# The order of three products in layer 0's LSTMs, and the engine of one copy

## The chip, the cores and the metric

One core of a Trainium2 chip runs the whole program. Its engines work side by side, each through its own queue of instructions: TensorE (PE in the profile, its weight loads PEld), VectorE (DVE), ScalarE (ACT), GpSimd (POOL), and the queues that issue DMAs (SP among them). Semaphores order what depends on another engine. The metric is the device time of one execution in microseconds; the time before is the median of three runs.

## The reference, cut to what matters

A stack of four graph layers works on x of shape (128, 64, 256): 128 sequences of 64 nodes with 256 features. The change lies in layer 0, in its LSTMs:

```python
for p in range(1, MAX_SKIP + 1):                     # MAX_SKIP = 4
    nw = Tv // p
    wins = h[:, :nw * p, :].reshape(Bv * nw, p, Hd)  # windows of p nodes
    last = _lstm_last(Wih[p - 1], Whh[p - 1], bih[p - 1], bhh[p - 1], wins)
    idx = jnp.arange(nw) * p + (p - 1)
    h = h.at[:, idx, :].set(last.reshape(Bv, nw, Hd))

def step(carry, x_t):                                # in _lstm_last
    h, c = carry
    g = x_t @ Wih.T + h @ Whh.T + bias
    i, f, gg, o = jnp.split(g, 4, axis=-1)
    c = sigmoid(f) * c + sigmoid(i) * tanh(gg)
    h = sigmoid(o) * tanh(c)
```

For each window length p = 1 to 4 an LSTM runs over windows of p nodes, from a zero state, and its last hidden state replaces the window's last node. The next p reads what the one before has written. Features and hidden state have 256 elements each, and a gate is a 256x256 product with x, and one with h from the second step on. All is in float32.

## The kernel before

**The work of the LSTMs.** Nodes stand in the free dimension, features in the partitions, in two blocks of 128. Nodes are split into two halves u as well, so a gate is a 2x2 by 2x2 block product. It is done with seven block products in place of eight (a Strassen scheme): `Weights` and `prepare` make sums of weight blocks and of input blocks, and numbers 1 to 7 name the products. `w` is the window length p. The batch goes in two halves of 64 sequences; in each, w runs from 1 to 4 (a phase), and a phase is cut into parts: four parts of N = 512 columns for w=1, four of 256 for w=2, two of 336 for w=3 and two of 256 for w=4. Two parts go hand in hand: step t of the one, then step t of the other. A step with t = 0 (a first step) has three gates (i, g, o) and takes one matmul a product; later steps have four (i, g, f, o) and two matmuls a product, the second with h. There are 24 + 48 + 112 = 184 gates: 8 steps of w=1, 16 first steps of w=2 to 4, 28 later steps. The program's order of matmuls is kept as it is written; for the other engines a scheduler, which works when the program is built, places independent instructions.

**A gate** (`gate`, a generator) yields three times and so has four parts:
- A: products 1 into `pa` and 2 into `pb`; ScalarE copies `pa` out (L684), VectorE adds `pb` (L685), ScalarE applies the function (in `func`, L669).
- B: product 6 onto `pa`, copied by ScalarE (L689); product 7 into `pc`, copied by ScalarE (L691): the third partial sum, block (1, 1).
- C: product 5 onto `pa`, which has to wait until L689 has read it; VectorE adds `pa` to the copied `pc` (L694).
- D: product 3 onto `pa`, which has to wait until L694 has read it, and a function straight from it; product 4 onto `pc`, added by VectorE (L699); a function on both remaining blocks; then `gate_done`.

PSUM has three banks for `pa`, three for `pc` and two for `pb`, which are also used to transpose a finished group (`group_out`, with the residual add L170).

`gate_done` multiplies i by g (L709, or L720 in a first step), updates c (L717, L718), takes its tanh (L721), and after the o gate makes h (L739) with the sums of its blocks (L741 to L743), or writes the result back to hT (L726 for w=1, L734 for a last step). `prepare` makes the next step's inputs: copies by ScalarE (L622, L623), subtractions by VectorE (L624, L630, L631; L613, L617, L618 for w=1). GpSimd makes the sums of the weight blocks in line 432.

**The loop over gates** is a software pipeline. In each slot one gate is new, the one before it is the middle gate (`flight[-1]`), and the one before that is the oldest:

```python
            if len(flight) > 1:
                next(flight[-1][1])          # middle gate: part C
                old = flight.pop(0)
                next(old[1], None)           # oldest gate: part D
```

Ahead of this the new gate does A, after it B. TensorE's order in a slot is so 1, 2 (new), 5 (middle), 3, 4 (oldest), 6, 7 (new).

Of the kernel before, what the change touches and what calls it, by code (L numbers as in the profile page):

```python
# [30 lines left out]
def gnn_stack_kernel(ctx: ExitStack, tc: tile.TileContext, a: dict, out: bass.AP):  # L31
    nc = tc.nc
# [24 lines left out]
    def token_tiles(ap, n=0):  # L57
        return ap[n * CHUNK : (n + 1) * CHUNK, :].rearrange("(i p) d -> p i d", p=P)
# [347 lines left out]
    with ExitStack() as l0:  # L406
# [178 lines left out]
        class Step:  # L585
# [90 lines left out]
            def gate(self, q):  # L676

                N = self.N
                pa = psl.tile([P, 512], F32, tag="pa", name="pa", bufs=3)
                pb = psl.tile([P, 512], F32, tag="bank", name="pb", bufs=2)  # L680
                pc = psl.tile([P, 512], F32, tag="pc", name="pc", bufs=3)
                self.product(q, ((1, pa, True), (2, pb, True)))
                blk, second = self.new_gate(q)
                nc.scalar.copy(blk[0, 0], pa[:, :N])  # L684
                nc.vector.tensor_tensor(blk[0, 0], pb[:, :N], blk[0, 0], ALU.add)  # L685
                self.func(q, blk[0, 0], blk[0, 0], 0)
                yield
                self.product(q, ((6, pa, False),))
                nc.scalar.copy(blk[1, 0], pa[:, :N])  # L689
                self.product(q, ((7, pc, True),))  # L690
                nc.scalar.copy(blk[1, 1], pc[:, :N])  # L691
                yield
                self.product(q, ((5, pa, False),))
                nc.vector.tensor_tensor(blk[1, 1], pa[:, :N], blk[1, 1], ALU.add)  # L694
                yield
                self.product(q, ((3, pa, False),))
                self.func(q, blk[0, 1], pa[:, :N], 0)
                self.product(q, ((4, pc, False),))
                nc.vector.tensor_tensor(blk[1, 0], pc[:, :N], blk[1, 0], ALU.add)  # L699
                self.func(q, second, second, 1)  # L700
                self.gate_done(q)
# [57 lines left out]
        def fetch_x(n):  # L759
            xt = xres.tile([P, 4, D], F32, tag="xres", name="xres")  # L760
            nc.sync.dma_start(out=xt, in_=token_tiles(a["x"], n))
            return xt
# [3 lines left out]
        def group_out(g, c):  # L766

            for u in range(2):
                n = 4 * g + 2 * u + c
                xt = residual.pop(n)  # L770
                for ip in range(2):
                    add_transposed(xt, 2 * ip, hTs0[g % 2][:, u], c * CHUNK + ip * 256)
                nc.gpsimd.dma_start(out=token_tiles(xa[n]), in_=xt)
                if g < 2:
                    m = n + NCH // 2
                    nc.sync.dma_start(
                        out=hTs0[g][:, u, :, c * CHUNK : (c + 1) * CHUNK], in_=hmem[m]
                    )

        def first_norms1(norms):  # L780

            for step in range(8):
                if step < 4:
                    for i in range(2):
                        norms[step // 2].stats(step % 2 * 2 + i)
                    if step % 2:
                        norms[step // 2].roots()
                else:
                    for i in range(2):
                        norms[step // 2 - 2].scaled(step % 2 * 2 + i)  # L790
                yield

        def phase_over(ph):

            if ph + 2 < len(phases):
                later_weights.append((slot + 8, ph + 2))
            nxt = ph + 1 if ph + 1 < len(phases) and phases[ph + 1] > 1 else ph + 2
            if phases[ph] > 1 and nxt < len(phases):
                weights["hh", nxt] = Weights("hh", phases[nxt])
# [3 lines left out]
        flight = []  # L803
# [3 lines left out]
        for slot in range(len(tasks) + 2):  # L807
            new = tasks[slot] if slot < len(tasks) else None
            if new:
                step = steps[new[0]]  # L810
                one = step.gate(new[1])
                next(one)
            if len(flight) > 1:
                next(flight[-1][1])
                old = flight.pop(0)
                next(old[1], None)
            elif flight and not new:
                old = flight.pop(0)
                next(old[1], None)
            else:  # L820
                old = None
                if flight:
                    next(flight[-1][1])
            if new:
                next(one)
                flight.append((new, one))
                at, k = new[0], new[2]
                while outs and outs[0][0] <= slot:
                    group_out(*outs.pop(0)[1:])

                new_half = at + 1 < len(steps) and at and steps[at + 1].w == 1 < step.w
                if k == len(step.gates) - (1 if new_half else 2) and at + 1 < len(steps):
                    steps[at + 1].prepare()
                if step.w == MAX_SKIP and step.t == 2 and k < 2:
                    for u in range(2):
                        n = 4 * step.g + 2 * u + k
                        later.append((slot, "x", n))
            while later and later[0][0] <= slot:
                _, kind, n = later.pop(0)
                residual[n] = fetch_x(n)  # L840
            next(norm_steps, None)
            while later_weights and later_weights[0][0] <= slot:
                _, ph = later_weights.pop(0)
                weights["ih", ph] = Weights("ih", phases[ph])
            if old:
                (at, q, k), step = old[0], steps[old[0][0]]
                if k == len(step.gates) - 1:
                    if at + 1 == len(steps) or steps[at + 1].phase != step.phase:
                        phase_over(step.phase)
                    if step.phase == len(phases) - 1 and step.t == 1 and step.g == NGR - 1:  # L850

                        t_ = wsp.tile([P, 2, 4, 2, P], F32, tag="wih", name="x_first", bufs=2)
                        flat = t_.rearrange("p k q j m -> p k (q j m)")
                        norms1 = {}
                        for n in range(2):
                            xt = flat[:, n, :].rearrange("p (i d) -> p i d", i=4)
                            nc.sync.dma_start(out=xt, in_=token_tiles(xa[n]))
                            norms1[n] = Norm(xt)
                        norm_steps = first_norms1(norms1)
                    if step.w == MAX_SKIP and step.t == MAX_SKIP - 1:  # L860
                        outs += [(slot + 1, step.g, 0), (slot + 2, step.g, 1)]
# [420 lines left out]
    with ExitStack() as l2:  # L1282
# [48 lines left out]
        with ExitStack() as dense2:  # L1331
# [62 lines left out]
            with ExitStack() as first_dense:  # L1394
# [39 lines left out]
                flight = []  # L1434
# [61 lines left out]
            def second_layer(pr, split):  # L1496
                parts = [({k: v[:, kb, :] for k, v in w2Q.items()}, Late(pr, kb), kb == 1) for kb in range(2)]

                n0, n1 = hs[2 * pr][0], hs[2 * pr + 1][0]
                dst = {(0, 0): n0[:, 0, :], (1, 0): n0[:, 1, :], (1, 1): n1[:, 0, :], (0, 1): n1[:, 1, :]}  # L1500

                def ready(j, u):
                    nc.vector.bn_stats(stats2[:, j, 2 * pr + u, :], dst[j, u])

                return quarters(parts, dst, ready, split)
# [8 lines left out]
            flight = [second_layer(0, True), second_layer(1, True)]  # L1514
# [281 lines left out]
```

## Time and profile before

| what | value |
|---|---|
| median of three runs | 2114.04 us (2113.0 to 2115.65) |
| the profiled execution, its own time | 2112.7 us |
| the profiled execution, span | 2110.9 us |
| LSTMs, products of line 641 | from 192 to 1274 us of the span |
| PE busy in 192 to 1287 us | 1066.2 of 1095 us |
| DVE and ACT busy there | 646.6 and 653.1 us |
| copy L691, 184 times | 76.5 us busy, 416 ns mean |
| copy L689, 184 times | 74.0 us busy, 402 ns mean |
| addition L694, 184 times | 87.4 us busy, 475 ns mean |

The span runs from the first to the last instruction that the profile shows; the execution's own time has some 1.8 us around it. A busy time is the union of an engine's instructions. In lists of waits the columns are: the engine and line that waited, whom it waited for, us in total, number of times, the longest. In a timeline each row has the start and the duration in us, engine, line, operation, tiles and shapes, how many instructions are merged in it, and, in brackets, how long the engine stood idle before it and what released it. Each matmul of the program shows as two records, and ends of matmuls are modelled, so starts are the better measure.

### The profile page before, as it was taken

The page shows a single profiled execution, that of the slowest core. Times are in us where ns is not written, and L with a number is a line of the kernel's source. Part 1 is how long each engine was busy: PE and PEld are TensorE (multiplying, and loading weights), DVE is VectorE, ACT ScalarE, POOL GpSimd, SP SyncE. Part 2 cuts the span into 40 slices and gives each one's busy share as a digit, 9 for nine tenths or more (in the row PEclk, how much of TensorE's full clock was granted, in tenths as well). Part 3 has the DMA queues.
Part 4 walks back from the last instruction along what each step waited for, and adds up shares of the span by engine and source line. Part 5 has one row for each costly group of instructions (what it writes and reads, how often), then busy time and mean ns, then how long its engine had stood idle before and what let it go on. Part 6 is the DMA issues. An engine that isn't in the chain of part 4 may idle for free.

```text
span 2110.9 us, 25487 instructions
## 1 busy us (share of the span) xinstructions
PE 2028.9 (96%) x9444; PEld 1348.2 (64%) x9444; DVE 1352.1 (64%) x2453; ACT 1186.4 (56%) x2264; POOL 309.1 (15%) x432
## 2 busy tenths in 40 slices
PE   8999999999999999999999998999999989999898
PEld 6776488766688746886668884333334665434686
DVE  8764665564655577556546555576676767786676
ACT  4354766654655467656456554565565356591444
POOL 3000000100200020002001002113312420000662
PEclk9999999999999999999999999999999999999899
DMA  9221000100100340001000006113234751022012
GB/s 315 88 95 50 0 21 1 41 0 1 40 1 1 120 159 20 1 1 40 1 11 30 1 22 203 60 41 104 67 90 131 230 189 60 0 70 90 30 61 70
DMA packets 94444, 135.06 MB, mean 64 GB/s; under 512 B 6384, under 2 KB 82032, under 8 KB 92144
## 3 DMA queue, kind: packets, MB, share of 16 engines
q1 hardware_dynamic: 87600, 109.11, 15.5%
q0 software_dynamic: 6112, 24.12, 3.8%
q8 instruction: 74, 1.21, 0.2%
q10 hardware_dynamic: 608, 0.20, 0.1%
q14 instruction: 50, 0.41, 0.1%
HBM read 87.28 MB, written 46.14 MB: 63 GB/s over the span
## 4 chain that ended last, share of the span: by engine, by line
PE 81%; ACT 6%; DVE 6%; issue 4%; DMA 2%; POOL 1%; SPq 0%; ACTq 0%; POOLq 0%; DVEq 0%
PE pa L641 24%; PE bank L50 20%; PE pc L641 12%; PE pair L50 6%; PE pb L641 6%; PE pa L1341 5%; PE pc L1341 2%; ACT gate L669 2%; PE bank L1132 1%; PE pb L1341 1%; ACT gate L721 1%; PE pair L1626 1%; DMA xo<-xa 1%; PE pair L1594 1%; DVE lstm_c L720 1%
## 5 line engine op out<-in xcount | busy, mean ns | idle before, releaser
L641 PE MATMUL pa<-xop,sih 128*128 128x256 f32 (+2 forms) x1056 | 346.6, 417 | 11.8 <-ACT gate L689 10.1
L669 ACT ACTIVATE gate<-gate,bias 128x256 f32<-128x256 f32 (+2 forms) x368 | 246.9, 678 | 181.0 <-DVE gate L685 97.4
L641 PEld LDWEIGHTS pa<-xop,sih 128*128 128x128 f32 x1056 | 198.5, 190 | 85.5 <-issue 20.9
L641 PE MATMUL pc<-xop,wih 128*128 128x256 f32 (+2 forms) x736 | 251.1, 423 | 0.0
L641 PE MATMUL pa<-lstm_h,shh 128*128 128x256 f32 (+1 forms) x672 | 212.7, 398 | 0.0
L963 DVE SCALAR_TENSOR_TENSOR lr<-lr 128x1024 f32<-128x1024 f32 x128 | 152.0, 1218 | 85.4 <-ACT lr L962 85.2
L685 DVE TENSOR_TENSOR gate<-pb,gate 128x256 f32<-128x256 f32 (+2 forms) x184 | 87.5, 475 | 162.1 <-PE pb L641 126.0
L641 PEld LDWEIGHTS pc<-xop,wih 128*128 128x128 f32 x736 | 139.8, 190 | 51.2 <-issue 22.5
L699 DVE TENSOR_TENSOR gate<-pc,gate 128x256 f32<-128x256 f32 (+2 forms) x184 | 87.4, 475 | 119.2 <-PE pc L641 117.7
L641 PEld LDWEIGHTS pa<-lstm_h,shh 128*128 128x128 f32 x672 | 127.7, 190 | 30.2
L962 ACT COPY lr<-pair 128x1024 f32<-128x1024 f32 x128 | 125.0, 1015 | 34.3 <-PE pair L50 34.3
L641 PE MATMUL pc<-lstm_h,whh 128*128 128x256 f32 (+1 forms) x448 | 141.8, 398 | 0.0
L684 ACT COPY gate<-pa 128x256 f32<-128x256 f32 (+2 forms) x184 | 76.9, 418 | 104.3 <-PE pa L641 103.6
L669 ACT ACTIVATE gate<-pa,bias 128x256 f32<-128x256 f32 (+2 forms) x184 | 94.8, 515 | 71.1 <-PE pa L641 70.1
L50 PE MATMUL pair<-sd_hot,xq 64*128 64x512 f32 x512 | 134.4, 622 | 0.3 <-ACT lr L962 0.3
L50 PE MATMUL bank<-wlv,hT 128*128 128x512 f32 x256 | 122.8, 611 | 7.0 <-ACT hT L154 7.0
L694 DVE TENSOR_TENSOR gate<-pa,gate 128x256 f32<-128x256 f32 (+2 forms) x184 | 87.4, 475 | 35.3 <-PE pa L641 33.1
L641 PE MATMUL pa<-xop,wih 128*128 128x256 f32 (+1 forms) x320 | 101.8, 400 | 5.4 <-ACT xop L622 3.1
L432 POOL TENSOR_TENSOR sih<-wih 128x512 f32<-128x512 f32 x8 | 10.8, 1350 | 632.2 <-DMA wih<-in_WihT 440.7
L641 PE MATMUL pb<-xop,wih 128*128 128x256 f32 (+1 forms) x320 | 100.5, 398 | 0.0
L641 PEld LDWEIGHTS pc<-lstm_h,whh 128*128 128x128 f32 x448 | 85.1, 190 | 20.1
L50 PEld LDWEIGHTS bank<-wlv,hT 128*128 128x128 f32 x256 | 44.8, 189 | 81.9 <-issue 62.1
(321 smaller groups left out, 3844.2 us busy)
## 6 DMA issues: line engine op xcount, KB each, us to landing
field<-sd_hot SPq DMA_DIRECT2D x8, 1152.0 KB, 10.4
wih<-in_WihT SPq DMA_DIRECT2D x8, 1024.0 KB, 5.0
xres<-in_x SPq DMA_DIRECT2D x16, 512.0 KB, 5.3
xa<-xres POOLq DMA_DIRECT2D x16, 512.0 KB, 4.6
xin<-xb SPq DMA_DIRECT2D x16, 512.0 KB, 3.9
h<-xb SPq DMA_DIRECT2D x16, 512.0 KB, 3.8
out_x<-h SPq DMA_DIRECT2D x16, 512.0 KB, 2.9
xin<-in_x SPq DMA_DIRECT2D x15, 512.0 KB, 5.9
```

Source lines behind the costliest of these rows:

```text
L50: nc.tensor.matmul(o, lhsT, rhs, start=start, stop=stop)
L641: ins = nc.tensor.matmul(p[:, : self.N], weights[kind, self.phase](k, q), x[k], start=first_ and kind == "ih", stop=kind == "hh" or not se ...
L669: nc.scalar.activation(out, in_, AF.Tanh if q == 2 else AF.Sigmoid, bias=bias[:, self.w - 1, 2 * q + j : 2 * q + j + 1],)
L684: nc.scalar.copy(blk[0, 0], pa[:, :N])
L685: nc.vector.tensor_tensor(blk[0, 0], pb[:, :N], blk[0, 0], ALU.add)
L694: nc.vector.tensor_tensor(blk[1, 1], pa[:, :N], blk[1, 1], ALU.add)
L699: nc.vector.tensor_tensor(blk[1, 0], pc[:, :N], blk[1, 0], ALU.add)
L720: nc.vector.tensor_tensor(c_, i_, g_, ALU.mult)
L721: nc.scalar.activation(g_, c_, AF.Tanh)
L962: nc.scalar.copy(lr, p)
L963: nc.vector.scalar_tensor_tensor(lr, lr, 0.2, lr, ALU.mult, ALU.max)
L1341: ins = nc.tensor.matmul(p, lhs[k], x[k], start=first_, stop=last_one, skip_group_check=True)
```

## The change

Two edits. In the slot of the pipeline the oldest gate does part D before the middle gate does part C: TensorE's order becomes 1, 2 (new), 3, 4 (oldest), 5 (middle), 6, 7 (new). And in a first step with w > 1 the copy of `pc` (the third partial sum) is a VectorE copy; for w = 1 and in later steps it stays on ScalarE.

```diff
@@ -688,7 +688,8 @@
                 self.product(q, ((6, pa, False),))
                 nc.scalar.copy(blk[1, 0], pa[:, :N])
                 self.product(q, ((7, pc, True),))
-                nc.scalar.copy(blk[1, 1], pc[:, :N])
+
+                (nc.vector.tensor_copy if not self.t and self.w > 1 else nc.scalar.copy)(blk[1, 1], pc[:, :N])
                 yield
                 self.product(q, ((5, pa, False),))
                 nc.vector.tensor_tensor(blk[1, 1], pa[:, :N], blk[1, 1], ALU.add)
@@ -811,9 +812,9 @@
                 one = step.gate(new[1])
                 next(one)
             if len(flight) > 1:
-                next(flight[-1][1])
                 old = flight.pop(0)
                 next(old[1], None)
+                next(flight[-1][1])
             elif flight and not new:
                 old = flight.pop(0)
                 next(old[1], None)
```

The added blank line moves the lines after it by one in the changed kernel's profile: L691 is L692 there, L694 is L695, L699 is L700, and so on.

## The prediction

> **What bounds the kernel now.** I read the page first: engines, then the 40 slices, then TensorE's waits, then a table of stretches, then the timeline at one wait.
>
> ```profile
> PE 2028.9 (96%) x9444; PEld 1348.2 (64%) x9444; DVE 1352.1 (64%) x2453; ACT 1186.4 (56%) x2264; POOL 309.1 (15%) x432
> ...
> PE pa L641 <- ACT gate L689: 10.1, 12, 1.5
> ...
> PE pa L641 <- ACT xop L622: 3.1, 2, 1.5
> ...
> PE pa L641 <- ACT gate L669: 2.1, 3, 1.0
> ...
> PE pa L641 <- ACT gate L684: 1.4, 4, 0.4
> ```
>
> TensorE is busy 96% of the span, so only its idle time can be won. All products of the LSTMs have line 641. TensorE waited there for ScalarE's copy L689 (the third product of a gate leaves `pa`) 10.1 us in 12 waits, and 6.6 us for three other ScalarE steps: 16.7 us, 0.8% of the span, is the most that the gates hold. Waits for VectorE's sum L694 don't occur in this list.
>
> The stretches (columns: length, then busy us of PE, PEld, DVE, ACT, POOL, granted clock, DMA share and rate):
>
> ```profile
> 268.00:286.00 18.00, 15.17 (x69) 12.69 (x68) 15.34 (x28) 14.91 (x35) 5.08 (x4) 1.00 0.17 59
> 337.00:354.00 17.00, 16.02 (x73) 13.45 (x72) 13.42 (x27) 14.66 (x35) 0.00 (x0) 1.00 0.00 1
> 408.00:432.00 24.00, 22.32 (x77) 13.98 (x76) 20.20 (x28) 18.49 (x36) 12.21 (x8) 1.00 0.20 82
> 560.00:580.00 20.00, 16.32 (x69) 12.08 (x68) 17.64 (x26) 15.31 (x32) 14.20 (x8) 1.00 0.23 97
> ```
>
> These are the four pairs of first steps with w > 1 in the first half of the batch (two of w=2, one each of w=3 and w=4); the second half repeats them. PE misses 2.83, 0.98, 1.68 and 3.68 us: 9.2 us, over half of the 16.7. In a first step each product is one matmul, not two, while ScalarE and VectorE have as much to do per gate. What the reader is to see: ScalarE isn't alone. VectorE is busy 85, 79, 84 and 88% of these stretches, and GpSimd, preparing weights, is busy beside it in all but the second.
>
> One wait, in the second stretch:
>
> ```profile
> 347.77 0.41 DVE L699 TENSOR_TENSOR gate<-pc,gate 128x256 f32<-128x256 f32 x1
> ...
> 348.42 1.11 ACT L669 ACTIVATE gate<-gate,bias 128x256 f32<-128x256 f32 x2
> ...
> 349.43 0.36 ACT L689 COPY gate<-pa 128x256 f32<-128x256 f32 x1
> 349.56 1.23 DVE L739 TENSOR_TENSOR lstm_h<-gate 128x1024 f32<-128x1024 f32 x1 [0.78 <-ACT gate L669]
> 349.68 0.38 ACT L691 COPY gate<-pc 128x256 f32<-128x256 f32 x1
> 349.84 1.13 PE L641 MATMUL pa<-xop,sih 128*128 128x256 f32 x4 [0.62 <-ACT gate L689]
> ```
>
> The fifth product of the middle gate stands 0.62 us because L689 is in ScalarE's queue behind two activations; the two last products of the oldest gate, behind it in TensorE's queue, need nothing that is late.
>
> **What the Trainium skill says.** "PSUM — Partial Sum Buffer", Engine vs sequencer instructions: ScalarE's and VectorE's queues are strict FIFO and matmuls start in program order. The trace agrees: in the wait just shown nothing overtakes. "SBUF — State Buffer", Who interferes with whom: a VectorE instruction with two SBUF inputs contends with a GpSimd instruction that reads SBUF, one with at most one doesn't. The trace agrees: L720 on 128x1024 or 128x1344 ranges from 1225 to 2528 ns, the long ones beside GpSimd's L432. "VectorE: DVE Perf Modes", Why PSUM operands drop a tier: an fp32 copy out of PSUM runs at 1x. So I price the moved copy like an addition from PSUM; the trace has 691 ns (median) for the 128x512 copy L145 and 684 for an L694 of that size.
>
> **The change part by part.**
>
> *The order.* Instruction counts stay the same; no DMA moves. In every slot products 3 and 4 of the oldest gate now stand ahead of product 5 of the middle one. In first steps a product of 256 columns takes 0.43 us (starts in the timeline), so 5 gets 0.86 us more for L689, 1.13 at 336 columns. The oldest gate ends one product earlier: 0.43 us in first steps, 0.86 later, and with it L699, the activation, and the cell state. In exchange product 3 loses slack: between a gate's 5 and its 3 stood seven products (3, 4, 6, 7, 1, 2, 5), now four (6, 7, 1, 2). That is 1.7 us instead of 3.0 in first steps, in which L694 must come through VectorE's queue. In later steps it is 3.4 instead of 6.0 us; TensorE has 6 us a slot there against some 3 for VectorE, so I charge nothing; if that cover goes, 28 such steps of four gates would show it.
>
> *The copies.* 16 first steps with w > 1, three gates each: 48 copies L691 leave ScalarE and join VectorE. ScalarE gains the 0.25 us from the start of L689 to that of L691 (349.43 to 349.68), 12 us in all; it is worth at most what of the 16.7 is left. VectorE gets 0.33 us each (L699 at 347.77, next start 348.10), 0.42 at most, so 2.0 to 2.5 us in a w=2 or w=4 pair and some 3 in w=3. On the table: 15.3+2.5 of 18, 13.4+2.5 of 17, 20.2+3 of 24, 17.6+2.5 of 20 us. VectorE then has 94 to 101% where it had 79 to 88. The copy lies before the next L685 in the queue, which feeds ScalarE, and before the next L694, which feeds TensorE.
>
> *By stretch.* I walked the changed queues by hand with the durations of the timeline.
> - 337 to 354: products 3 and 4 fill the waits of 0.36 and 0.62; L684, which 6 waits for, comes earlier since L691 has left. At the end 3 finds L694 some 0.25 late behind the four operations that make h. Gain 1.0.
> - 268 to 286: VectorE's L726, L624 and the slow L720 (2.33) stand before L694; 3 waits about 0.6 twice where 5 waited 1.35 and 1.49. Gain 1.1 of 2.83.
> - 408 to 432: 3 must now wait for the L694 that stood between L739 and L741. It goes behind L739 (2.67 beside GpSimd), L630, L741, L631, L742, L685, L743 and L699: 1.5 late. The early waits are filled for 0.9. Loss 0.6.
> - 560 to 580: the same place, with L739 2.18 and L741 1.42: L694 ends near 580.1, where 3 could start at 578.3. Together with L694 behind L624, L699 and L630 near 565 the loss is 1.3.
> Per half -1.0 -1.1 +0.6 +1.3 = -0.2, twice -0.4.
>
> *The ends.* At the last step TensorE waits 5.5 us for L734. The gate before the last ends 0.86 earlier and so its cell state; the last gate's own chain doesn't move. I take 0.6. Between the halves VectorE waits for a DMA into hT (2.52 us at 722.2), which hides all but some 0.4. Sum: -1.0; bounds 0 and -1.7.
>
> Total -1.4 us. The profiled execution's span is 2110.9 and its own time 2112.7; minus 1.4 is 2111.3 for that execution. The median of the runs shown is 1.3 above it, so the predicted median is 2112.6. Each stretch may be wrong by 1 us or so, and the halves err alike: about 4 us to either side.
>
> **The rivals.** About 4.2 us, 0.2%, is what a measurement of this kernel can tell from no change.
> - *Even (the forecast):* the wait for L689 becomes one for L694, a little shorter in w=2, longer in w=3 and w=4. For it: VectorE's 79 to 88%. 2112.6, from 2110 to 2118.
> - *Faster: VectorE keeps up*, because the earlier end of the oldest gate pulls its chain forward too and a copy fits in its gaps. Then each wait for L689 shrinks by up to 0.86: twelve waits of 1.35, 1.49, 0.36, 0.62, 0.24, 1.38 and the second half's like them lose 7.4, the ends 1.0: -8.4, 2105.6. If the freed ScalarE also clears the rest, -17, 2097. Against it: VectorE's queue at h.
> - *Slower: VectorE becomes the bound beside GpSimd.* Place: w=3 and w=4 first steps. Price: their 24 copies at 0.51 and 0.42 all add to the path, 5.6 a half, 11.2, less the w=2 gains of 4.2 and 1.0 of the ends: +6, 2120. It decides once VectorE's work with the copies fills the stretch, which the table puts at 97 and 101% there.
> - That the scheduler moves the work back: in the built program's queues 5 does stand behind 4 and 48 copies do stand on VectorE; no chance of its own.
>
> **How the numbers follow.** Even 0.40, faster 0.37 (the nearest part just past 4.2 us, the far one to -12), slower 0.23. The likeliest gives 2112.6; 2104 to 2121 leaves about a tenth out on either side: it takes in the -8.4 case and the +6 case with 1 us or so beyond each.
>
> **What would show it.** Right: TensorE's waits on L689 fall from 10.1 to under 4 us while waits on L694 appear, 4 us or more, near the h operations of w=3 and w=4; VectorE over 90% in those stretches; L699 of later steps 0.86 earlier and no new wait there. Wrong: no waits on L694 and PE idle down in all four stretches (then faster), or waits on L694 or L685's activation beyond 15 us, or in later steps (then slower).

## The result and the profile after

The changed kernel takes 2112.74 us (median of 22 runs, 2109.75 to 2116.25), the kernel before, run beside it, 2115.64 us (22 runs, 2112.71 to 2119.4). The ratio is 0.9986 with a 95% interval of 0.9979 to 0.9992: 2.9 us less, under the 4.2 us that count as a difference here. The predicted time was 2112.6.

The profiled execution shows a span of 2111.4 us, 0.5 more than that of before, although its LSTMs end about 3 us earlier. What was won there is lost in the later layers, which the change doesn't touch: they last 836.6 us from the last product of line 641 on before, and 839.5 after. One profile can't show 3 us on its whole span, so the traces below are read inside the LSTMs. The engines, from the page:

```profile
PE 2035.0 (96%) x9444; PEld 1352.2 (64%) x9444; DVE 1364.0 (65%) x2501; ACT 1176.4 (56%) x2216; POOL 309.7 (15%) x432
```

48 instructions have moved from ACT to DVE. TensorE's waits in the changed kernel's LSTMs (whom it waited for, us in total, times, longest):

```profile
PE pa L641 <- DVE gate L695: 8.8, 11, 1.6
...
PE bank L165 <- DVE hT L735: 4.3, 1, 4.3
PE pa L641 <- ACT gate L684: 3.1, 4, 1.2
PE pa L641 <- ACT xop L622: 2.7, 2, 1.3
PE pb L641 <- DVE gate L685: 0.4, 1, 0.4
```

The list has no L689 any more. Where it had 10.1 us for L689 it now has 8.8 us for L695, VectorE's addition that was L694 and stood nowhere in the list of before. The others fell together from 6.6 to 6.2: L669's 2.1 us went, L684 rose from 1.4 to 3.1. The four stretches of first steps, with the columns explained in the prediction:

```profile
268.00:286.00 18.00, 17.14 (x77) 13.83 (x76) 16.16 (x34) 14.85 (x32) 6.08 (x4) 1.00 0.17 59
337.00:354.00 17.00, 16.94 (x79) 14.52 (x79) 14.15 (x32) 13.87 (x32) 0.00 (x0) 1.00 0.01 1
408.00:432.00 24.00, 21.82 (x76) 13.78 (x75) 20.37 (x30) 16.93 (x31) 13.89 (x8) 1.00 0.07 29
560.00:580.00 20.00, 15.68 (x67) 11.86 (x66) 18.57 (x31) 13.76 (x27) 12.83 (x8) 1.00 0.11 46
```

TensorE gains 1.97 and 0.92 us in the two stretches of w=2 and loses 0.50 and 0.64 in those of w=3 and w=4. The last two are the ones in which GpSimd is busy longest. The timeline of the changed kernel shows the place of the longest wait, in w=3:

```profile
419.40 1.82 DVE L740 TENSOR_TENSOR lstm_h<-gate 128x1344 f32<-128x1344 f32 x1
...
419.76 2.59 POOL L432 TENSOR_TENSOR shh<-whh,shh 128x512 f32<-128x512 f32 x1
...
421.14 1.57 DVE L630 TENSOR_TENSOR xop<-xop 128x336 f32<-128x336 f32 x1
...
422.63 0.84 DVE L742 TENSOR_TENSOR lstm_h<-lstm_h 128x672 f32<-128x672 f32 x1
...
424.66 0.49 DVE L744 TENSOR_TENSOR lstm_h<-lstm_h 128x336 f32<-128x336 f32 x1
...
425.07 0.50 DVE L700 TENSOR_TENSOR gate<-pc,gate 128x336 f32<-128x336 f32 x1
425.49 0.49 DVE L695 TENSOR_TENSOR gate<-pa,gate 128x336 f32<-128x336 f32 x1
...
426.04 0.83 PE L641 MATMUL pa<-xop,sih 128*128 128x336 f32 x2 [1.56 <-DVE gate L695]
```

VectorE runs without a gap from 419.40 to L695, and L695 is last in the row. Product 3 waits 1.56 us for it. One subtraction, L630, takes 1.57 us beside GpSimd's L432; its sister L631, an equal operation later in the same row, takes 0.50. GpSimd's L432 ends at 422.35, ahead of L631.

### The profile page after: what moved, and what is told of

It is laid out like the page before. It is cut to its first block, busy times and chain, and to the rows that moved or that the text cites. A ratio compares the mean times of both kernels' runs of the same rounds, so it can differ in the third digit from the quotient of the medians.

```text
span 2111.4 us, 25481 instructions
## 1 busy us (share of the span) xinstructions
PE 2035.0 (96%) x9444; PEld 1352.2 (64%) x9444; DVE 1364.0 (65%) x2501; ACT 1176.4 (56%) x2216; POOL 309.7 (15%) x432
## 4 chain that ended last, share of the span: by engine, by line
PE 86%; DVE 6%; ACT 4%; issue 1%; DMA 1%; POOL 1%; SPq 0%; ACTq 0%; POOLq 0%; DVEq 0%
PE pa L641 25%; PE bank L50 20%; PE pc L641 12%; PE pair L50 6%; PE pb L641 6%; PE pa L1342 5%; PE bank L1133 3%; PE pc L1342 2%; PE pb L1342 1%; ACT gate L669 1%; PE pair L1113 1%; PE bank L165 1%; PE pair L1627 1%; PE pair L1595 1%; ACT gate L722 1%
## 5 line engine op out<-in xcount | busy, mean ns | idle before, releaser
L669 ACT ACTIVATE gate<-gate,bias 128x256 f32<-128x256 f32 (+2 forms) x368 | 247.3, 679 | 174.0 <-DVE gate L685 91.1
L685 DVE TENSOR_TENSOR gate<-pb,gate 128x256 f32<-128x256 f32 (+2 forms) x184 | 87.7, 477 | 225.5 <-PE pb L641 153.9
L700 DVE TENSOR_TENSOR gate<-pc,gate 128x256 f32<-128x256 f32 (+2 forms) x184 | 87.7, 477 | 119.9 <-PE pc L641 119.5
L684 ACT COPY gate<-pa 128x256 f32<-128x256 f32 (+2 forms) x184 | 75.9, 412 | 96.6 <-PE pa L641 96.2
L695 DVE TENSOR_TENSOR gate<-pa,gate 128x256 f32<-128x256 f32 (+2 forms) x184 | 87.6, 476 | 44.0 <-PE pa L641 43.4
L669 ACT ACTIVATE gate<-pa,bias 128x256 f32<-128x256 f32 (+2 forms) x184 | 93.8, 510 | 26.9 <-PE pa L641 25.2
L689 ACT COPY gate<-pa 128x256 f32<-128x256 f32 (+2 forms) x184 | 75.3, 409 | 59.2 <-PE pa L641 57.9
L432 POOL TENSOR_TENSOR sih<-wih 128x512 f32<-128x512 f32 x8 | 10.8, 1350 | 625.0 <-DMA wih<-in_WihT 625.0
```

What stands on the lines that cost most here:

```text
L669: nc.scalar.activation(out, in_, AF.Tanh if q == 2 else AF.Sigmoid, bias=bias[:, self.w - 1, 2 * q + j : 2 * q + j + 1],)
```

## The experiments

Three theories stood after the result. **T1**: the order fills the waits for L689 and turns them into waits for VectorE, where GpSimd's sums stretch VectorE's work; the copies matter little. **T2**: the gain is ScalarE's relief by the copies, the order is nearly nothing. **T3**: the order brings a larger gain, and the copies give part of it back. Each ratio below is against runs of the kernel before made beside it, whose medians were 2114.52 to 2115.40 us.

### One edit at a time

The first kernel is the changed one with its copy line put back:

```diff
-                (nc.vector.tensor_copy if not self.t and self.w > 1 else nc.scalar.copy)(blk[1, 1], pc[:, :N])
+                nc.scalar.copy(blk[1, 1], pc[:, :N])
```

> The new order alone; the copy of pc stays on ScalarE everywhere. T1 (the order trades waits for L689 against waits for VectorE's addition, and the copies matter little either way): 1 to 3 us under the kernel before; no waits on L689, some 6 to 9 us of waits on the addition in the first steps of w=3 and w=4, the 1.56 us wait of w=3 shortened by about the 0.3 us of one copy. T2 (the gain comes from the relief of ScalarE): no gain, -0.5 to +1 us, with waits on ScalarE's L684 and L669 of 5 us or more. T3 (the order brings the gain and the copies take part of it back): -4 to -5 us, faster than both.

Measured: 2111.04 us, ratio 0.9983 (0.9976 to 0.9989), 3.5 us under before. Its waits:

```profile
PE pa L641 <- DVE gate L695: 5.9, 10, 1.5
...
PE pa L641 <- ACT xop L622: 1.9, 2, 1.0
PE pb L641 <- DVE gate L685: 1.9, 1, 1.9
PE pb L641 <- ACT xop L622: 1.2, 2, 0.6
...
PE pa L641 <- ACT gate L689: 0.2, 1, 0.2
```

The second has the copy line and the old order:

```diff
                 next(flight[-1][1])
                 old = flight.pop(0)
                 next(old[1], None)
```

> The old order with the 48 copies on VectorE. T1: 0 to -1.5 us against the kernel before; the waits on L689 stay at 8 us or more, since L689 stands behind activations and not behind L691; the waits on L684 (1.4 us) shrink. T2: -2.5 to -3 us, waits on L689 halved. T3: +1 to +2 us, with waits on VectorE's addition appearing in the old order too.

Measured: 2116.51 us, ratio 1.0006 (0.9996 to 1.0016). Its waits:

```profile
PE pa L641 <- ACT gate L689: 9.7, 13, 1.4
...
PE pa L641 <- DVE gate L694: 0.7, 2, 0.5
```

T2 falls: without the new order the copies bring nothing, and the waits for L689 stay, because L689 stands behind activations and the copy that left stood behind L689. The whole gain is in the order: 3.5 us, a little more than the 1 to 3 us that T1 gave.

Between T1 and T3 the times can't decide. Order alone, with 0.9983, and order with copies, with 0.9986, can't be told apart. The copies alone came out 1.3 us above before by the ratio, where T3 had +1 to +2 and T1 0 to -1.5, but the interval takes in no change; T3's waits for L694 in the old order did show, 0.7 us. The one trace of each kernel leans to T3: with the order alone TensorE waits 11.1 us for the gates, with the copies as well 15.0, and from the first to the last product the LSTMs take 1076.1 and 1079.3 us. T3's -4 to -5 us for the order alone was not reached. So in this setting the copies bring no gain; that they cost something is likely from the traces and not shown by the times.

T1's forecast that the longest wait would shorten by a copy's 0.3 us failed: it is still 1.5 us. There the product L740 took 2.24 us beside GpSimd in place of 1.82, which took back the missing copy.

### Without the sums of the weight blocks

In both orders, line 432 was changed:

```diff
-                    nc.gpsimd.tensor_tensor(o, x, y, op)
+                    nc.gpsimd.memset(o, 0.0)
```

> The changed kernel, except that GpSimd writes zeros where it made the sums of the weight blocks: these sums are left out of the computation, GpSimd reads nothing from SBUF for them. T1 (the new waits on the addition come from VectorE operations stretched beside GpSimd's sums): the waits on the addition of 8.8 us fall to under 4, VectorE's operations on 128x1024 take about 1.23 us everywhere in w=3 and w=4, and the time is 5 us or more under that of the changed kernel, further under than the old order gains from the same edit. Rival (VectorE's queue itself is too long and GpSimd doesn't matter): the waits stay within 2 us of 8.8, the time within 2 us of the changed kernel.

> The kernel before, with the same edit (the sums of the weight blocks are left out, zeros are written). T1: the waits on L689 stay at 8 us or more, since ScalarE doesn't suffer from GpSimd; the time is 1 to 3 us under the kernel before, and the new order with the copies is 6 us or more faster than this one. Rival: the distance between the orders stays at the 3 us that it has with the sums.

Measured: the changed kernel with this edit takes 2099.88 us, ratio 0.9925 (0.9911 to 0.9940); the kernel before with it takes 2110.95 us, 0.9983 (0.9976 to 0.9991). The order and the copies, worth 2.9 us with the sums, are worth 11 us without them. Of both gains 1.6 to 1.8 us lie ahead of the LSTMs, whose first product starts that much earlier. Waits in the changed kernel without sums:

```profile
PE pa L641 <- ACT xop L622: 2.7, 2, 1.3
PE pa L641 <- ACT gate L684: 1.5, 2, 0.8
PE pa L641 <- DVE gate L695: 1.2, 3, 0.6
```

and in the kernel before without sums:

```profile
PE pa L641 <- ACT gate L689: 7.6, 12, 1.3
```

The waits for L695 fall from 8.8 to 1.2 us. GpSimd's sums cause them. The old order hardly notices, since it waits for ScalarE at those places; its waits for L689, 7.6 us, and its gain of 3.6 us by the ratio both lie a little outside what T1 had forecast (8 or more, 1 to 3). ScalarE isn't stretched: in the changed kernel its 128x672 activation took 0.84 us beside a sum (at 417.35 us) and 0.85 us with none (at 425.60). Whether it is GpSimd's reading or its mere activity isn't separated here: in the stretch from 408 to 432 us GpSimd was busy 13.89 us in the changed kernel and 0.53 us without the sums, so both went.

### VectorE's queue rearranged

The sums of h's blocks and the last two subtractions of `prepare` are put into functions of their own and called after part C of the middle gate, so that L695 stands ahead of them. The edit acts in all steps with w > 1, not in first steps alone:

```diff
                 old = flight.pop(0)
                 next(old[1], None)
                 next(flight[-1][1])
+                at = flight[-1][0][0] + 1
+                if at < len(steps) and steps[at].v is not None:
+                    steps[at].prepared()
+                if steps[old[0][0]].h is not None:
+                    steps[old[0][0]].sums_of_h()
```

> The changed kernel, with VectorE's queue rearranged in first steps: the last two subtractions of the next step's inputs and the three that make the sums of h's blocks are issued after the addition that TensorE's product 3 waits for; GpSimd's sums stay. If the place of the addition in VectorE's queue behind the h chain is what holds product 3: the 1.56 us waits of w=3 fall under 0.5 us, those of w=4 by half, 3 to 5 us less than the changed kernel. If it is VectorE's throughput beside GpSimd, and not the order in its queue: the wait only moves to the products that need h or the inputs (L622, L685 or L641 on lstm_h), and the time stays within 1.5 us of the changed kernel.

Measured: 2107.61 us, ratio 0.9967 (0.9955 to 0.9978), 7.6 us under before and 4 to 5 under the changed kernel. L695 is L700 here:

```profile
PE pa L646 <- DVE gate L700: 3.4, 10, 0.8
...
PE pa L646 <- DVE lstm_h L745: 0.8, 1, 0.8
```

The place in the queue holds the addition too, not only the throughput: 8.8 us became 3.4 with the sums where they were. A new wait for h itself (its product, L740 before the lines moved) shows once, 0.8 us.

### The sums moved to where VectorE has slack

Here nothing is left out, so no product works on zeros in place of weights. The sums of the input weights are issued four slots later (not those that fall into a phase with w=1), and a copy of one column makes them wait for h of a first step, so that GpSimd makes them beside later steps. The recurrent weights' sums stay, since their one buffer is needed until the phase before is over.

```diff
+                if after is not None:
+                    late(nc.gpsimd.tensor_copy(s[:, 0, 0, :1], after))
                 for o, x, y, op in (
...
-                later_weights.append((slot + 8, ph + 2))
+                later_weights.append((slot + (12 if phases[ph + 1] > 1 else 8), ph + 2))
...
-                weights["ih", ph] = Weights("ih", phases[ph])
+                weights["ih", ph] = Weights(
+                    "ih", phases[ph], steps[at].state["h"][1][:, :1] if steps[at].t else None
+                )
```

> The changed kernel, with all sums computed, but those of the input weights are held back by a one-column copy that reads h of the first step, so that GpSimd makes them beside later steps (where VectorE has slack) and only the recurrent weights' sums stay in the first steps. If the stretch of VectorE beside GpSimd is the cause: 5 to 9 us less than the changed kernel, 8 to 12 less than before; sums seen after 290, 430 and 830 us. If TensorE's gain without the sums came from something else that vanished with them (the matmuls' own waits for weights, SBUF traffic of TensorE's loads): within 2 us of the changed kernel.

Measured: 2102.39 us, ratio 0.9937 (0.9923 to 0.9951): 10.4 us under the changed kernel by the two ratios, a little more than expected. The waits for the addition, L697 here, fall from 8.8 us:

```profile
PE pa L643 <- DVE gate L697: 1.9, 5, 0.6
```

The timeline at the same place, lines moved by two:

```profile
418.18 1.81 DVE L742 TENSOR_TENSOR lstm_h<-gate 128x1344 f32<-128x1344 f32 x1
...
419.91 0.49 DVE L632 TENSOR_TENSOR xop<-xop 128x336 f32<-128x336 f32 x1
...
423.19 0.49 DVE L697 TENSOR_TENSOR gate<-pa,gate 128x336 f32<-128x336 f32 x1
...
423.73 0.83 PE L643 MATMUL pa<-xop,sih 128*128 128x336 f32 x2 [0.49 <-DVE gate L697]
```

GpSimd ended its sums at 418.57. The subtraction that took 1.57 us takes 0.49, the row is 1.08 us shorter, and the wait is 1.07 us shorter: the same operations in the same order, one neighbour gone.

The same move was then made in the three other combinations: the new order without copies, the old order, and the old order with copies.

> The new order without the VectorE copies, with the input weights' sums beside later steps. If the copies cost only because VectorE is stretched there: now they should help, and this kernel is 1 to 3 us slower than the one with the copies, with waits on L684 and L669. If they never mattered: within 1 us of it.

> The kernel before, with the input weights' sums beside later steps (nothing left out). With the sums in their old place the two edits gave 3 us; with them moved, order and copies together stand 13 us under before. If moving the sums is a gain of its own (whatever the order): -8 to -10 us here. If it pays only once TensorE waits for VectorE, as the theory has it: -1.5 to -4 us, with the waits on L689 still 8 us or more, and the two edits are worth 9 to 11 us in this setting.

> The old order with the 48 VectorE copies and with the input weights' sums beside later steps. In the new order the copies gain about 3 us in this setting. If that gain is ScalarE's relief as such: the same 3 us under the old order without copies. If in the old order L689 sets the wait and stands ahead of the moved copy: within 1.5 us of the old order without copies.

| ratio to before (95% interval) | sums in their place | input weights' sums later |
|---|---|---|
| old order | 1 | 1.0000 (0.9992 to 1.0009) |
| old order, copies on VectorE | 1.0006 (0.9996 to 1.0016) | 0.9996 (0.9987 to 1.0004) |
| new order | 0.9983 (0.9976 to 0.9989) | 0.9951 (0.9937 to 0.9966) |
| new order, copies (the change) | 0.9986 (0.9979 to 0.9992) | 0.9937 (0.9923 to 0.9951) |

The table is the answer to all three expectations. Moving the sums gains nothing in the old order: even the 1.5 us expected at least did not come, and its waits for L691, the old L689, are still there:

```profile
PE pa L643 <- ACT gate L691: 8.9, 12, 1.4
```

In the changed kernel the same move leads to 13 us under before. The copies gain in one corner only, the new order with the sums away: 2102.39 us (2100.20 to 2103.25) with them, 2106.51 us (2103.18 to 2107.17) without. The two ratios' intervals meet at 0.9951 and hardly more, so those 3 to 4 us are likely but not firm. Part of it shows in the waits: without the copies TensorE waits 2.8 us for ScalarE's activation, and with them not at all.

```profile
PE pa L643 <- ACT gate L671: 2.8, 3, 1.2
```

### Both rearrangements

> Both rearrangements of the two kernels before it. If they cure the same waits: no more than 1 us under the better of the two. If they cure different ones: their gains add, 10 us or more under the changed kernel.

Measured: 2098.48 us (2096.32 to 2100.99), ratio 0.9919 (0.9905 to 0.9933): 16.7 us under the kernel before and the lowest median of the kernels that keep the whole computation. From the changed kernel's 0.9986, the queue brought 0.0019 alone, the sums 0.0049, both 0.0067. By these figures the gains add, but each ratio is uncertain by some 0.0013, so the times don't show it, and since the sums alone bring 10 us, the mark of 10 us can't tell either. The one trace of each kernel says that the two cure largely the same waits: those for VectorE's addition fall from 8.8 us to 3.4 with the queue, 1.9 with the sums and 1.1 with both, and the LSTMs take 1079.3 us from first to last product in the changed kernel, 1071.4 with the queue, 1067.9 with the sums and 1067.1 with both. What is left of TensorE's waits for the gates:

```profile
PE pa L648 <- ACT xop L625: 2.7, 2, 1.3
PE pa L648 <- DVE gate L702: 1.1, 3, 0.6
PE pa L648 <- ACT gate L696: 0.7, 2, 0.4
```

That is 4.5 us where the kernel before had 16.7 and the changed one 15.0.

## Why the prediction was right, and where it wasn't

**The time** was right, 2112.6 against 2112.74, but that closeness is luck. The change was forecast at -1.4 us and measured at -2.9; the kernel before, on whose 2114.04 us the forecast was built, came out at 2115.64 in the runs beside the changed one, which made up for the difference. Between the profiles of before and after the starts of TensorE's products, taken ahead of and behind each pair, give:

| | predicted, us | first half | second half |
|---|---|---|---|
| w=2, first pair | -1.1 | -1.5 | -0.6 |
| w=2, second pair | -1.0 | -1.2 | -1.2 |
| w=3 | +0.6 | +0.3 | +0.4 |
| w=4 | +1.3 | +0.4 | +0.7 |
| sum of the stretches, both halves | -0.4 | | -2.6 |
| the ends | -1.0 | | -0.3 |

All eight signs are right; the gain in w=2 was priced a little low, the loss in w=3 and w=4 and the gain at the ends too high. **The mechanism** held at its place: product 3 of w=3 was to come 1.5 us late behind L739, L630, L741, L631, L742, L685, L743 and L699, and it came 1.56 late behind these eight. That the size fits is in part luck: the sums' stretch was expected on L739, 2.67 us, with L630 at 0.50; L740 took 1.82 and L630 1.57. L689's waits were to fall under 4 us and went altogether; waits for L694 were to be 4 us or more and are 8.8. In later steps the addition of product 4 was to come 0.86 us earlier: it starts 2.16 us (median) after the newest gate's L684, where it was 3.02.

**One reading was too small.** The 9.2 us that TensorE misses in the four stretches of the first half were set against the 16.7 us of waits of both halves, as "over half". Taken one by one, all 16.7 us of these waits lie in the four stretches and their four repetitions.

**The term that was too large** is the loss in w=4. The 1.3 us took L739 at 2.18 and L741 at 1.42 from before. In the changed kernel the counterparts L740 and L742 took 1.97 and 0.68:

```profile
572.35 0.42 DVE L692 COPY gate<-pc 128x256 f32<-128x256 f32 x1
...
572.68 1.97 DVE L740 TENSOR_TENSOR lstm_h<-gate 128x1024 f32<-128x1024 f32 x1
...
574.91 0.68 DVE L742 TENSOR_TENSOR lstm_h<-lstm_h 128x512 f32<-128x512 f32 x1
```

The order shifts VectorE's operations against GpSimd's sums, and which of them is stretched changes. Of the two waits that were named, the one near 565 came (1.41 us at 564.64, for L695 behind L630), and the one at 578.3 did not. The largest that was not foreseen, 1.14 us for L684, has ScalarE's copies L622 and L623 ahead of it, not VectorE:

```profile
571.36 1.12 ACT L622 COPY xop<-hT 128x512 f32<-128x512 f32 x1
...
572.39 0.65 ACT L623 COPY xop<-hT 128x256 f32<-128x256 f32 x1
...
572.94 0.36 ACT L684 COPY gate<-pa 128x256 f32<-128x256 f32 x1
...
573.35 0.70 PE L641 MATMUL pa<-xop,sih 128*128 128x256 f32 x2 [1.14 <-ACT gate L684]
```

"L684 comes earlier since L691 has left" was so argued for the second pair of w=2 and doesn't carry to w=4: there the copy had not been what stood before L684.

**VectorE's share** was put at 94 to 101% and came out at 90, 83, 85 and 93%; the sign "over 90%" for w=3 and w=4 so failed in w=3. The price of a copy was right: behind the copy L692 of 256 columns at 572.35 us the next operation starts 0.33 us later, and behind one of 336 columns at 418.99 us 0.41. The step that failed is the sum: for w=2 and w=4 it took the upper price of 0.42, and it added the copies to unchanged work in a fixed window, while the window holds other operations once the order has changed. With the order alone VectorE's busy time in the second stretch fell from 13.42 to 12.71 us, and the six copies brought it to 14.15.

**The ends.** L734 was priced at -0.6, and its wait did fall from 5.5 to 4.3 us. But the last gate's product 3 now waits 0.59 us for L695 at 1270.3 us, so half of it was paid back a few us earlier. No other later step shows a wait for L695, so the charge of nothing for those was right.

**The rivals.** "Slower: VectorE becomes the bound" needed a filled stretch, and none was. "Faster: VectorE keeps up" was put at -8.4 us: the runs with the sums moved show what that case would have been, -13 us with the copies and -10 without, and that GpSimd stood in its way. "VectorE's queue at h", my reason against it, was part of the cause: rearranging the queue was worth some 4 us by itself and moving the sums 10, and in the traces the two overlap.

## What to carry to other kernels

A reordering that fills one engine's wait is worth only what the next engine in line leaves, so walk that engine's queue up to what is waited for now, and look at which neighbours stretch it. Measure an edit together with the edit that frees its next limit: here three edits were worth 3.5 us, nothing and nothing by themselves, and 13 together. If work on a side engine has no deadline, tie it by a data dependence to a stretch where the engine it disturbs has slack; a later place in the program had not held it back, as the sums were issued eight slots after a phase's end and still ran in first steps (the later place of twelve slots without the copy was not run).

## What the hardware showed that was not expected

- The same 128x336 subtraction of two SBUF tiles took 0.49 us alone and 1.57 us beside a GpSimd sum, and that sum 2.59 us where its undisturbed ones take 1.27: both engines pay, though not each time, since another L630 of this size, at 408.19 us, started 0.11 us ahead of a sum and took 0.51. The Trainium skill's "SBUF — State Buffer", Who interferes with whom, names the contention of a VectorE instruction that has two SBUF inputs with a GpSimd instruction that reads SBUF, and the trace agrees: in the kernel with the sums moved, the addition L697, which has one operand in PSUM, kept its 0.49 us at 417.35 us, beside a sum that ran from 416.40 to 418.57. In the changed kernel the 22 additions and copies of 128x336 with one operand in PSUM that lay beside sums for at least 60% of their time took 0.49 to 0.51 us. That one with at most one SBUF input doesn't contend, the page says of instructions outside the two-port modes; the prediction left this proviso out, and no run here shows those modes.
- Price by the step to the next start, not by the duration: a 128x256 VectorE copy shows 0.42 us, and in a queue that runs on the next operation starts 0.33 us after it. VectorE's busy time from 192 to 1287 us grew by a little less, 0.29 to 0.34 us for each of the 48 copies (14.1 us in the new order, 15.5 in the new order with the sums moved and 16.3 in the old order), since the same window holds somewhat different work in each kernel.
